# An AdaLN block in one kernel: summing the weights' lower halves on ScalarE in the set-up, and a new order for modulation, transfers and GpSimd work

## The chip, the core and the metric

The kernel runs on one core of one Trainium2 chip. The time is the device time of one execution in microseconds (us), the median of several runs; the profile is one further execution with the hardware profiler on.

## What is computed

The input `x` holds 4 batches of 2048 tokens with 256 channels. Six modulation rows come from a small matrix product, and two sub-layers follow: a chunked delta-rule memory with 4 heads of 64 channels, and a gated feed-forward network (FFN) with hidden layers of 1024.

```python
mod = (silu(c) @ wmod).reshape(4, 6, 1, 256)          # sa, ca, ga, sb, cb, gb
ga, gb = (sign * max(abs, 0.25) of each)
h = layernorm(x) * (1 + ca) + sa
# memory: per head, chunks of 64 tokens, keys rk = h / |h|, wk = rk one token later
A = inv(I + strict_tril(wk wk^T * decay))             # 64 x 64, each chunk and head
v_new = A v - (A wk) S ;  o = rk_g S + intra v_new ;  S = gamma^64 S + wk_g v_new
x = x + ga * (h + (alpha * o) @ Wr.T)
h = layernorm(x) * (1 + cb) + sb
# FFN, weights ternary (-1, 0, 1), scales per output column
f = silu(h W1 s) * (h W2 s); f = gelu(f H1 s); f = gelu(f H2 s)
out = x + gb * (f W3 s)
```

## The kernel before

**Tiling.** A chunk step `s` (0 to 31) holds 64 tokens of all four batches, as 128 partitions by 2 by 256. Two steps make a pair `g` (0 to 15). FFN `g` works on the 512 tokens of pair `g` and runs on TensorE; in its gaps the memory of the next pair is computed, in an order that a small planner (`Beside`, with assumed costs and due times) fixes when the kernel is built. Everything ahead of FFN 0 is the **set-up**: it computes the memory of pair 0 and prepares pair 1, loads weights, and decides one branch.

**The branch.** FFN weights are multiplied in one pass when the lower 16 bits of every fp32 weight are zero, as they are for ternary values. The set-up looks at all of them: `parts` lists 22 pieces of 512 KB (w1, w2, w3, 8 of h1, 8 of h2). `fetch` loads a piece into a staging tile `st`, on ScalarE's queue (ACTq). `look` has ScalarE copy the lower halves to a bf16 tile `low`, which TensorE multiplies by `ones` and adds up in the PSUM row `bad` (two matmuls a piece). `keep` writes an h1 or h2 piece to DRAM (`fh`) in rows of 512 bytes, so that FFN blocks can later be loaded as contiguous tiles `w<-fh`. `bulk` does one of each. At the end `some` and `flag` are formed from `bad`, and every engine loads `flag` and branches.

**The inverse of a pair** goes through four steps. `local_begin` writes `E` to DRAM (`d<-E`) and reads it back as `U` (`U<-d`), both on SyncE's queue (SPq). 31 calls of `local_inverse` (the rows, DVE instructions on `zt` and `Z`) invert blocks of 32. `local_blocks` writes `Z` to DRAM and reads it back (`d<-Z`, `E<-d`, on SPq). `local_diagonal` (`Dm`), `local_merge1` (`yp`, `Y`) and `local_merge2` (`ep`, `E`) finish.

**The recurrence** of a step is `rec_values` (TensorE `V`, ScalarE `vn`), `rec_update` (TensorE `new`, DVE `S` and `oT`), `rec_state` of the next step (TensorE `R` and `O`, DVE `v`), `rec_out` (TensorE `ap_`) and `rec_gain` (DVE `ga`, `y`). `moments` and `ffn_norm` make the FFN's input in `firsts` (tiles named `rkg` and `Dm`); `turn` transposes it (`tpf`) into `hs`. The memory's own inputs are made by `begin`, `local_units` (GpSimd `rk`), `local_keys` (TensorE `tp`), `local_values` (TensorE `vp`), `local_shift` (DMA `wkg<-rk` on SPq), `local_grams` (TensorE `G`, DVE `E` and `IT`), and by GpSimd in `local_residual` (`gh`, `y`), `local_reads` (`rkg`) and `local_writes` (`wkg`).

**What sets the order.** Each engine runs its instructions in one order, fixed at build time. `with stage():` puts its contents behind the last instruction that each engine had been given; inside a stage, and for instructions that are not the last, a scheduler orders. Each queue (SPq, ACTq) issues in its order, and its transfers start in that order. Every DMA also takes one of eight semaphores in turn, and is issued only when the DMA that had that semaphore before it has landed, whichever queue that was on. The tile ring `st` has 10 buffers.

One piece of code matters for the gate in front of the transfers. `first` is a small copy of a result, made only to hold back what stands behind it on ScalarE:

```python
act.copy(first, U[P - K:P, 0, :])
fetch(4)
```

Of the kernel before, what the change touches and what calls it, by code (L numbers as in the profile page):

```python
# [29 lines left out]
F32 = mybir.dt.float32  # L30
# [10 lines left out]
P = 128  # L41
# [48 lines left out]
def adaln_block_kernel(ctx: ExitStack, tc: tile.TileContext, x_in, ww, wr, decay, log_alpha, w1, w2, h1, h2, w3, scol,  # L90
# [80 lines left out]
    def move(out, in_):  # L171
        sp.dma_start(out=out, in_=in_)
# [289 lines left out]
    class Ffn:  # L462
# [151 lines left out]
    with tc.tile_pool(name="setup", bufs=1) as su:  # L614
# [11 lines left out]
        move(out=sk, in_=consts[:, KEPT:NCONST])  # L626
        move(out=kept, in_=consts[:, 0:KEPT])
        move(out=dec[:, 1, :], in_=log_alpha.partition_broadcast(P))
        move(out=wm[1], in_=wmv[:, :, 2 * D:4 * D])
        load(2)  # L630
        move(out=wwT, in_=ww.rearrange("(k p) o -> p k o", p=P))

        parts = [(t, w, k) for t, w in ((fw1, w1), (fw2, w2)) for k in range(NK)]
        parts += [(fw3, w3, k) for k in range(0, NH, 4)] + [(fhs[n], w, k) for n, w in enumerate((h1, h2)) for k in range(NH)]
        staged, seen, gone = [], [], []

        def fetch(count):
            for n in range(count):
                t = su.tile([P, HID], F32, tag="st", name="st", bufs=10)
                _, w, k = parts[len(staged)]  # L640
                staged.append(t)
                k2 = HID // w.shape[1]
                act.dma_start(out=t.rearrange("q (k o) -> q k o", k=k2),
                              in_=w[P * k:P * (k + k2), :].rearrange("(k p) o -> p k o", p=P))

        bad = pf.tile([1, 512], F32, tag="f", name="bad")
        ones = su.tile([P, 1], BF, name="ones")
        dve.memset(ones, 1.0)

        def look(count):  # L650

            for n in range(len(seen), len(seen) + count):
                seen.append(n)
                with stage():
                    low = su.tile([P, HID], BF, tag="low", name="low", bufs=2)
                    act.copy(low, staged[n].bitcast(U16).rearrange("q (o e) -> q o e", e=2)[:, :, 0])
                    for m in range(2):
                        pe.matmul(bad, lhsT=ones, rhs=low[:, 512 * m:512 * m + 512], start=n == 0 and m == 0,
                                  stop=n == len(parts) - 1 and m == 1)

        def keep(count):

            for n in range(count):
                at_ = 6 + len(gone)
                to, w, k = parts[at_]
                gone.append(at_)
                with stage():
                    act.dma_start(out=to[:, :, k, :].rearrange("o p c -> p o c"),
                                  in_=staged[at_].rearrange("q (o c) -> q o c", c=P))

        def bulk(count, more=1):
            for n in range(count):
                look(1)
                keep(1)
                with stage():
                    fetch(min(more, len(parts) - len(staged)))

        def part(at_, n):
            return sk[:, at_ - KEPT:at_ - KEPT + n]
# [18 lines left out]
        def modulation(j):  # L698

            got = []  # L700
            for n in range(2):
                ps = pf.tile([P, 2, D], F32, tag="f", name="ps_mod")
                for k in range(NK):
                    pe.matmul(ps, lhsT=rows(n, k), rhs=wm[j][:, k, :], start=k == 0, stop=k == NK - 1)
                got.append(ps)
            return got
# [53 lines left out]
            got = moments(2)  # L760
        with stage():
            local_values(1, hT1)
        look(8)
        with stage():
            rn = begin(2, got)
        with stage():
# [6 lines left out]
        with stage():  # L773
            first = su.tile([K, K], F32, name="first")
            act.copy(first, U[P - K:P, 0, :])
            fetch(4)
            move(out=wm[2], in_=wmv[:, :, 4 * D:6 * D])
            load(3)
            move(out=wrT[:, 0], in_=wr.rearrange("(k p) o -> p k o", p=P))
            for h in range(2):  # L780
                move(out=wrT[C * (1 - h):C * (1 - h) + C, 1], in_=wr.rearrange("(k h p) o -> h p k o", h=2, p=C)[h])
            s3b = su.tile([P, D], F32, name="s3b")
            move(out=s3b, in_=s3.partition_broadcast(P))
            move(out=sc, in_=scol)
# [10 lines left out]
        with stage():  # L795
            for n, ps in enumerate(modulation(1)):
                act.copy(mod[:, GA, n, :], ps[:, 0, :])
                act.copy(mod[:, SB, n, :], ps[:, 1, :])
        keep(2)
        with stage():  # L800
            hT = local_keys(2, hids[2])
        with stage():
            for n, ps in enumerate(modulation(2)):
                act.activation(mod[:, CB, n, :], ps[:, 0, :], AF.Identity, bias=1.0)
                act.copy(mod[:, GB, n, :], ps[:, 1, :])
        bulk(4, 0)

        def bounded(to):

# [10 lines left out]
        with stage():  # L820
            for n in range(2):
                bounded(mod[:, GA, n, :])
            local_writes(0)
            local_writes(1)
            local_reads(1)
        with stage():
            for n in range(2):
                bounded(mod[:, GB, n, :])
            dve.tensor_tensor(mod[:, GB], mod[:, GB], over(s3b, 1, 2), ALU.mult)
            local_residual(0, hids[0])  # L830
        with stage():
            got = moments(3)
# [1 line left out]
                for n in range(2):  # L834
                    dve.tensor_scalar(wrT[:, n, p, :], wrT[:, n, p, :], alc[:, n, p:p + 1], None, ALU.mult)
        with stage():
            local_diagonal()
            act.copy(first[:, 0:1], Dm[0:K, 1, 7, K - 1:K])
            fetch(6)
        with stage():  # L840
            Y = local_merge1()
        with stage():
            local_merge2(Y)
        bulk(1)
        with stage():
            vn = rec_values(0)
            rn = begin(3, got)
            local_residual(1, hids[1])
        bulk(1)
        with stage():  # L850
            oT = rec_update(0, vn, None)
            local_shift(2)
            local_units(3, hid, rn)
        with stage():
            oT1 = rec_state(1)
        bulk(1)
        with stage():
            vn = rec_values(1)
        with stage():
            a = rec_out(0, oT)  # L860
        with stage():
            rec_gain(0, a, dve)
        with stage():
            oT = rec_update(1, vn, oT1)
        bulk(1)
        with stage():
            got = moments(0)
            local_values(2, hT)
        with stage():
            hT = local_keys(3, hid)  # L870
        with stage():
            a = rec_out(1, oT)
        with stage():
            local_grams(2)
            local_shift(3)
        bulk(1)
        with stage():
            rec_gain(1, a, dve)
        with stage():
            ffn_norm(0, got, firsts[0])  # L880
        bulk(len(parts) - len(seen))
        with stage():
            got = moments(1)
            local_grams(3)
        with stage():
            ffn_norm(1, got, firsts[1])
            local_begin()
            local_residual(2, hids[2])
        with stage():
            local_values(3, hT)  # L890
            local_reads(3)
            local_writes(2)
            local_writes(3)
            local_residual(3, hid)
        some = su.tile([1, 1], F32, name="some")
        dve.tensor_reduce(some, bad, AX.X, ALU.add)
        dve.tensor_scalar(flag, some, 0.0, None, ALU.is_gt)

    val = nc.values_load(flag, min_val=0, max_val=1)

# [9 lines left out]
    class Beside:  # L910
# [14 lines left out]
        def __init__(self, exact, fp, done):  # L925
            self.exact, self.fp, self.hs, self.had = exact, fp, None, {}
            self.t, self.dve, self.act, self.limit, self.gated, self.taken, self.ahead = 0.0, 0.0, 0.0, None, False, False, False
            self.free = {"a1": [0.0], "a2": [0.0, 0.0]}
            self.done = dict.fromkeys(done, -20.0) | {("begin", 1): -4.0}
            self.todo = []  # L930
            for g in range(NP):
                self.pair(g)
            self.todo.sort(key=lambda e: self.RANK.index(f"{e[0][0]}{e[0][1] % 2}" if e[0][0] in ("state", "units") else e[0][0]))
# [133 lines left out]
    SET_UP += [(kind, s) for s in range(2) for kind in ("state", "V", "update", "out", "gain", "fmom", "norm", "turn")]  # L1067
    SET_UP += [("reads", s) for s in (0, 1, 3)] + [("merge2", 0), ("begin", 1)]

    def steps(exact):  # L1070
        for e in engines:
# [66 lines left out]
```

## Time and profile before

| | us |
|---|---|
| median of 3 runs (lowest to highest) | 1753.31 (1750.13 to 1756.47) |
| the profiled execution: its time | 1755.09 |
| its span (first to last instruction) | 1753.3 |
| set-up, until FFN 0's first matmul | 122.9 |
| TensorE busy in the set-up | 64.2 |
| TensorE busy in the 1630.4 behind it | 1602.1 |

A line of the profile names the engine (PE is TensorE, PEld its weight loads, DVE VectorE, ACT ScalarE, POOL GpSimd; SPq and ACTq are issues of DMA), the source line (nearly always 82, the helper that records every operation, so tiles tell instructions apart), the operation, and the tiles as out<-in. TensorE is nearly always busy behind the set-up and half idle in it.

### The profile page before, as it was taken

To read this page: it belongs to the slowest core of one execution; us is meant where nothing else is said; L and a number is where in the kernel's file an instruction comes from. 1 tells how busy PE (TensorE), PEld (TensorE's weight loads), DVE (VectorE), ACT (ScalarE), POOL (GpSimd) and SP (SyncE) were. 2 spreads that over 40 slices of the span, in tenths; PEclk is the share of its full clock that TensorE was granted. 3 is DMA by queue.
4 is the path that set the end of the run, shared out by engine and by line. 5 is a ranking of instruction groups with operands and counts; after the bars stand their busy time and mean duration, and the time that the engine had idled before them with its cause. 6 is when DMAs were issued, how large, how long until landed. Compare 5 with 4: busy or idle time off the path is not lost.

```text
span 1753.3 us, 36864 instructions
## 1 busy us (share of the span) xinstructions
PE 1666.3 (95%) x15236; PEld 1351.2 (77%) x15236; DVE 1001.5 (57%) x2414; ACT 729.9 (42%) x1199; POOL 534.7 (30%) x483
## 2 busy tenths in 40 slices
PE   5379999999999999999999999999999999999998
PEld 2157867878888887888888788888878888887887
DVE  5748484754646566474655657465664746555422
ACT  4334443444444444344443434344343444434342
POOL 3233324141342243324323332422333243231120
PEclk8679999999999999999999999999999999999999
DMA  7765333343433425243352534335253433525142
GB/s 211 235 180 144 92 89 95 94 121 120 131 109 92 140 61 167 82 126 107 96 142 61 158 90 126 110 83 150 64 157 92 116 114 86 146 65 150 61 133 86
DMA packets 189874, 205.46 MB, mean 117 GB/s; under 512 B 112576, under 2 KB 147520, under 8 KB 189696
## 3 DMA queue, kind: packets, MB, share of 16 engines
q10 hardware_dynamic: 57712, 154.68, 28.4%
q1 hardware_dynamic: 131984, 48.32, 12.6%
q8 instruction: 122, 2.00, 0.5%
q14 instruction: 56, 0.46, 0.1%
HBM read 169.40 MB, written 25.17 MB: 111 GB/s over the span
## 4 chain that ended last, share of the span: by engine, by line
PE 88%; DVE 5%; DMA 3%; ACT 1%; issue 1%; SPq 1%; POOL 0%; ACTq 0%; DVEq 0%; POOLq 0%
PE ps L82 70%; PE vp L82 3%; PE new L82 2%; DVE Z L82 2%; PE tp L82 2%; DVE zt L82 2%; PE V L82 1%; PE R L82 1%; PE ep L82 1%; PE G L82 1%; DVE raw L82 1%; PE O L82 1%; DMA d<-Z 1%; PE tpf L82 1%; PE yp L82 1%
## 5 line engine op out<-in xcount | busy, mean ns | idle before, releaser
L82 PE MATMUL ps<-act,w 128*128 128x512 f32 x4096 | 987.4, 396 | 14.8 <-DVE act L82 13.7
L82 PEld LDWEIGHTS ps<-act,w 128*128 128x128 f32 x4096 | 759.8, 188 | 181.0 <-DVE act L82 19.7
L82 ACT ACTIVATE raw<-ps,sc 128x512 f32<-128x512 f32 x384 | 264.7, 689 | 634.8 <-PE ps L82 629.2
L82 DVE TENSOR_TENSOR act<-raw,act 128x512 fp32r<-128x512 f32 x272 | 195.2, 718 | 218.1 <-ACT act L82 215.9
L82 ACT CAST act<-raw 128x512 fp32r<-128x512 f32 x384 | 237.7, 619 | 56.8 <-DVE raw L82 48.8
L82 PE MATMUL ps<-hs,fw 128*128 128x512 f32 x1024 | 246.5, 399 | 3.6 <-DVE raw L82 2.6
L82 PEld LDWEIGHTS ps<-hs,fw 128*128 128x128 f32 x1024 | 191.0, 189 | 53.7 <-DVE raw L82 5.6
L82 POOL TENSOR_TENSOR act<-raw,act 128x512 fp32r<-128x512 f32 x112 | 143.3, 1295 | 130.9 <-ACT act L82 130.9
L82 DVE TENSOR_TENSOR Z<-Z,zt 128x126 f32<-128x126 f32 (+22 forms) x496 | 161.9, 326 | 17.2
L82 DVE SCALAR_TENSOR_TENSOR raw<-ps,sc,raw 128x512 f32<-128x512 f32 x128 | 95.9, 749 | 110.7 <-PE ps L82 55.5
L82 POOL TENSOR_TENSOR rs<-rs,half 128x2 f32<-128x2 f32 x64 | 51.5, 805 | 338.9 <-DVE rs L82 338.2
L82 DVE TENSOR_TENSOR zt<-Z,U 128x126 f32<-128x126 f32 (+22 forms) x496 | 138.4, 279 | 16.4 <-DMA U<-d 4.5
L82 PE MATMUL ps<-fw,act 128*128 128x256 f32 x1024 | 125.6, 280 | 1.4 <-DVE act L82 1.4
L82 PEld LDWEIGHTS ps<-fw,act 128*128 128x128 f32 x1024 | 122.8, 188 | 4.0 <-DVE act L82 2.7
L82 POOL TENSOR_TENSOR y<-y,gb 128x512 f32<-128x512 f32 x30 | 39.5, 1318 | 234.6 <-DVE gb L82 234.6
L82 POOL TENSOR_TENSOR rn<-rn,half 128x8 f32<-128x8 f32 x32 | 53.9, 1683 | 141.0 <-DVE rn L82 140.3
L82 DVE SCALAR_TENSOR_TENSOR S<-S,gC,new 128x256 f32<-128x256 f32 x64 | 27.8, 476 | 84.3 <-PE new L82 84.3
L82 DVE BATCH_NORM_STATS2 bs<-y 128x6 f32<-128x256 f32 x128 | 47.8, 414 | 42.9 <-POOL y L82 37.0
L82 ACT ACT_TABLE_LOAD x35 | 44.9, 1283 | 64.0 <-PE ps L82 50.6
L82 PE MATMUL vp<-wwT,hT 128*128 128x256 f32 x256 | 65.8, 401 | 4.8 <-DMA wwT<-in_ww_dram 4.8
L82 POOL TENSOR_TENSOR rk<-hid,rn 128x512 f32<-128x512 f32 x32 | 34.8, 1087 | 99.2 <-DMA wkg<-rk 97.9
L82 POOL TENSOR_TENSOR y<-y,ga 128x512 f32<-128x512 f32 x30 | 40.2, 1340 | 78.2 <-DVE ga L82 78.2
(205 smaller groups left out, 1377.1 us busy)
## 6 DMA issues: line engine op xcount, KB each, us to landing
w<-fh ACTq DMA_DIRECT2D x256, 512.0 KB, 3.7
y<-in_x_dram SPq DMA_DIRECT2D x64, 128.0 KB, 4.2
st<-in_h_dram ACTq DMA_DIRECT2D x16, 512.0 KB, 5.9
U<-d SPq DMA_DIRECT2D x32, 256.0 KB
fh<-st ACTq DMA_DIRECT2D x16, 512.0 KB, 6.2
out_dram<-y SPq DMA_DIRECT2D x64, 128.0 KB, 2.4
wkg<-rk SPq DMA_DIRECT2D x64, 126.0 KB
d<-E SPq DMA_DIRECT2D x64, 64.0 KB, 1.9
```

Of the source, the lines that this page charges most:

```text
L82: made = make(*args, **kwargs)
```

## The change

It touches the set-up, the list of what the planner takes as done, and one due time.

- `look`: ScalarE's instruction adds up along each partition as it copies (`accum_out`), into a column of `sums`; the 44 `bad` matmuls become two small ones with `sums`, and `low` becomes six tiles.
- `wm[1]`, 512 KB for modulation rows, is loaded behind `local_begin`'s stage instead of early. `modulation(2)` stands behind the 31 rows and `local_blocks`; bounding `GB` stands behind `rec_values(1)`.
- `st` gets 12 buffers. The pieces of h1 behind the first 12 are loaded and kept on SPq, behind `local_blocks`; the pieces of h2 are loaded and looked at, but their copy to `fh1` goes from DRAM to DRAM, eight transfers on SPq in the last stage.
- The order of the recurrence and of steps 2 and 3 changes: `local_values(2)` and `local_keys(3)` stand ahead of `rec_out(0)`; both `local_grams` together.
- `local_residual(3)`, `local_writes(2)`, `local_writes(3)`, `local_reads(3)` are left to the planner, which puts them at the start of FFN 0. `begin` of pair 1 counts as done at -2 instead of -4.

```diff
-        move(out=wm[1], in_=wmv[:, :, 2 * D:4 * D])
...
-        def fetch(count):
+        def fetch(count, by=act.dma_start):
...
-                t = su.tile([P, HID], F32, tag="st", name="st", bufs=10)
+                t = su.tile([P, HID], F32, tag="st", name="st", bufs=12)
...
-                    low = su.tile([P, HID], BF, tag="low", name="low", bufs=2)
-                    act.copy(low, staged[n].bitcast(U16).rearrange("q (o e) -> q o e", e=2)[:, :, 0])
-                    for m in range(2):
-                        pe.matmul(bad, lhsT=ones, rhs=low[:, 512 * m:512 * m + 512], start=n == 0 and m == 0,
-                                  stop=n == len(parts) - 1 and m == 1)
+                    act.activation(lows[n % 6], staged[n].bitcast(U16).rearrange("q (o e) -> q o e", e=2)[:, :, 0],
+                                   AF.Copy, accum_out=sums[:, n:n + 1])
...
-        look(8)
+        look(6)
...
             act.copy(first, U[P - K:P, 0, :])
             fetch(4)
+            move(out=wm[1], in_=wmv[:, :, 2 * D:4 * D])
             move(out=wm[2], in_=wmv[:, :, 4 * D:6 * D])
...
-        keep(2)
+        keep(4)
         with stage():
             hT = local_keys(2, hids[2])
-        with stage():
-            for n, ps in enumerate(modulation(2)):
...
-        bulk(4, 0)
+        look(3)
...
         with stage():
+            local_diagonal()
+            act.copy(first[:, 0:1], Dm[0:K, 1, 7, K - 1:K])
+            fetch(4, move)
+        keep(2, move)
+        with stage():
+            fetch(2, move)
+        with stage():
+            Y = local_merge1()
             local_residual(0, hids[0])
...
         with stage():
             oT = rec_update(0, vn, None)
             local_shift(2)
             local_units(3, hid, rn)
+            local_residual(2, hids[2])
+        look(1)
+        keep(2, move)
+        with stage():
+            fetch(4, move)
...
         with stage():
             vn = rec_values(1)
+        look(2)
+        with stage():
+            for n in range(2):
+                bounded(mod[:, GB, n, :])
+            dve.tensor_tensor(mod[:, GB], mod[:, GB], over(s3b, 1, 2), ALU.mult)
+        with stage():
+            local_values(2, hT)
+        with stage():
+            hT = local_keys(3, hid)
+        look(6)
...
-        bulk(len(parts) - len(seen))
         with stage():
             got = moments(1)
-            local_grams(3)
+            local_values(3, hT)
+        with stage():
+            pe.matmul(bad[:, 6:len(parts)], lhsT=ones, rhs=sums[:, 6:], start=True, stop=True)
         with stage():
             ffn_norm(1, got, firsts[1])
+        some = su.tile([1, 1], F32, name="some")
+        with stage():
+            dve.tensor_reduce(some, bad[:, 0:len(parts)], AX.X, ALU.add)
+            dve.tensor_scalar(flag, some, 0.0, None, ALU.is_gt)
+        with stage():
             local_begin()
-            local_residual(2, hids[2])
-        with stage():
-            local_values(3, hT)
-            local_reads(3)
-            local_writes(2)
-            local_writes(3)
-            local_residual(3, hid)
...
+            for k in range(NH):
+                move(out=fhs[1][:, :, k, :], in_=h2[k * P:(k + 1) * P, :].rearrange("p (o c) -> o p c", c=P))
...
-            self.done = dict.fromkeys(done, -20.0) | {("begin", 1): -4.0}
+            self.done = dict.fromkeys(done, -20.0) | {("begin", 1): -2.0}
...
-        "load", "mom", "hidden", "squares", "sizes", "units", "residual", "keys", "values", "shift", "writes", "gram")]
+        "load", "mom", "hidden", "squares", "sizes", "units", "keys", "values", "shift", "gram")]
+    SET_UP += [("residual", s) for s in range(3)]
...
```

Built, the change gives these orders, which the diff alone does not show. On ACTq the four `fetch(4)` transfers stand ahead of the `first` copy that reads `U`. On SPq the eight `fh1<-h2` transfers stand behind `local_shift(3)` and ahead of pair 1's `d<-E`. Behind the branch TensorE's order is the same as before; on DVE the inverse's rows of pair 1 begin one `raw` instruction later.

More of the change, by code (lines that the diff above doesn't have):

```diff
@@ L634, in adaln_block_kernel @@
         parts += [(fw3, w3, k) for k in range(0, NH, 4)] + [(fhs[n], w, k) for n, w in enumerate((h1, h2)) for k in range(NH)]
-        staged, seen, gone = [], [], []
-        def fetch(count):
+        staged, seen, known, gone = [], [], [], []
+        def fetch(count, by=act.dma_start):
             for n in range(count):
-                t = su.tile([P, HID], F32, tag="st", name="st", bufs=10)
+                t = su.tile([P, HID], F32, tag="st", name="st", bufs=12)
                 _, w, k = parts[len(staged)]
@@ L642, in fetch, with keep @@
                 k2 = HID // w.shape[1]
[L643 to L648, printed above, removed]
+                by(out=t.rearrange("q (k o) -> q k o", k=k2),
+                   in_=w[P * k:P * (k + k2), :].rearrange("(k p) o -> p k o", p=P))
+        ones = su.tile([P, 1], F32, name="ones")
+        lows = [su.tile([P, HID], BF, name=f"low{n}") for n in range(6)]
+        sums = su.tile([P, len(parts)], F32, name="sums")
+        dve.memset(sums, 0.0)
         def look(count):
             for n in range(len(seen), len(seen) + count):
+                with stage():
+                    act.activation(lows[n % 6], staged[n].bitcast(U16).rearrange("q (o e) -> q o e", e=2)[:, :, 0],
+                                   AF.Copy, accum_out=sums[:, n:n + 1])
                 seen.append(n)
-                with stage():
-                    low = su.tile([P, HID], BF, tag="low", name="low", bufs=2)
-                    act.copy(low, staged[n].bitcast(U16).rearrange("q (o e) -> q o e", e=2)[:, :, 0])
-                    for m in range(2):
-                        pe.matmul(bad, lhsT=ones, rhs=low[:, 512 * m:512 * m + 512], start=n == 0 and m == 0,
-                                  stop=n == len(parts) - 1 and m == 1)
-        def keep(count):
+        def keep(count, by=act.dma_start):
             for n in range(count):
@@ L667, in keep @@
                 with stage():
[L668 to L674, printed above, removed]
-                with stage():
-                    fetch(min(more, len(parts) - len(staged)))
+                    by(out=to[:, :, k, :].rearrange("o p c -> p o c"),
+                       in_=staged[at_].rearrange("q (o c) -> q o c", c=P))
         def part(at_, n):
@@ L798, in adaln_block_kernel @@
                 act.copy(mod[:, SB, n, :], ps[:, 1, :])
-        keep(2)
+        keep(4)
         with stage():
             hT = local_keys(2, hids[2])
-        with stage():
-            for n, ps in enumerate(modulation(2)):
-                act.activation(mod[:, CB, n, :], ps[:, 0, :], AF.Identity, bias=1.0)
-                act.copy(mod[:, GB, n, :], ps[:, 1, :])
-        bulk(4, 0)
+        look(3)
         def bounded(to):
@@ L820, in adaln_block_kernel @@
         with stage():
+            pool.memset(ones, 1.0)
+        bad = pf.tile([1, 512], F32, tag="f", name="bad")
+        with stage():
+            pe.matmul(bad[:, 0:6], lhsT=ones, rhs=sums[:, 0:6], start=True, stop=True)
+        with stage():
+            for n, ps in enumerate(modulation(2)):
+                act.activation(mod[:, CB, n, :], ps[:, 0, :], AF.Identity, bias=1.0)
+                act.copy(mod[:, GB, n, :], ps[:, 1, :])
+        with stage():
             for n in range(2):
@@ L826, in adaln_block_kernel @@
         with stage():
-            for n in range(2):
-                bounded(mod[:, GB, n, :])
-            dve.tensor_tensor(mod[:, GB], mod[:, GB], over(s3b, 1, 2), ALU.mult)
+            local_diagonal()
[6 more added lines that the diff above has]
+            Y = local_merge1()
             local_residual(0, hids[0])
@@ L836, in adaln_block_kernel @@
         with stage():
[L837 to L842, printed above, removed]
             local_merge2(Y)
-        bulk(1)
+            local_residual(1, hids[1])
         with stage():
@@ L847, in adaln_block_kernel @@
             rn = begin(3, got)
-            local_residual(1, hids[1])
-        bulk(1)
         with stage():
@@ L853, in adaln_block_kernel @@
             local_units(3, hid, rn)
+            local_residual(2, hids[2])
[3 more added lines that the diff above has]
+            fetch(4, move)
         with stage():
             oT1 = rec_state(1)
-        bulk(1)
         with stage():
             vn = rec_values(1)
+        look(2)
[5 more added lines that the diff above has]
+            local_values(2, hT)
+        with stage():
+            hT = local_keys(3, hid)
+        look(6)
         with stage():
@@ L864, in adaln_block_kernel @@
             oT = rec_update(1, vn, oT1)
-        bulk(1)
+        with stage():
+            local_shift(3)
         with stage():
             got = moments(0)
-            local_values(2, hT)
-        with stage():
-            hT = local_keys(3, hid)
+            masks = [local_grams(2, False), local_grams(3, False)]
         with stage():
             a = rec_out(1, oT)
+            ffn_norm(0, got, firsts[0])
         with stage():
-            local_grams(2)
-            local_shift(3)
-        bulk(1)
+            for n in range(2):
+                for m in range(2):
+                    masks[n](m)
+        look(22 - len(seen))
         with stage():
@@ L879, in adaln_block_kernel @@
         with stage():
-            ffn_norm(0, got, firsts[0])
-        bulk(len(parts) - len(seen))
+            got = moments(1)
+            local_values(3, hT)
         with stage():
-            got = moments(1)
-            local_grams(3)
+            pe.matmul(bad[:, 6:len(parts)], lhsT=ones, rhs=sums[:, 6:], start=True, stop=True)
         with stage():
             ffn_norm(1, got, firsts[1])
-            local_begin()
-            local_residual(2, hids[2])
-        with stage():
-            local_values(3, hT)
-            local_reads(3)
-            local_writes(2)
-            local_writes(3)
-            local_residual(3, hid)
-        some = su.tile([1, 1], F32, name="some")
-        dve.tensor_reduce(some, bad, AX.X, ALU.add)
-        dve.tensor_scalar(flag, some, 0.0, None, ALU.is_gt)
+        some = su.tile([1, 1], F32, name="some")
+        with stage():
+            dve.tensor_reduce(some, bad[:, 0:len(parts)], AX.X, ALU.add)
+            dve.tensor_scalar(flag, some, 0.0, None, ALU.is_gt)
+        with stage():
+            local_begin()
+            for k in range(NH):
+                move(out=fhs[1][:, :, k, :], in_=h2[k * P:(k + 1) * P, :].rearrange("p (o c) -> o p c", c=P))
     val = nc.values_load(flag, min_val=0, max_val=1)
@@ L1065, in adaln_block_kernel @@
     SET_UP = [(kind, s) for s in range(4) for kind in (
-        "load", "mom", "hidden", "squares", "sizes", "units", "residual", "keys", "values", "shift", "writes", "gram")]
-    SET_UP += [(kind, s) for s in range(2) for kind in ("state", "V", "update", "out", "gain", "fmom", "norm", "turn")]
-    SET_UP += [("reads", s) for s in (0, 1, 3)] + [("merge2", 0), ("begin", 1)]
+        "load", "mom", "hidden", "squares", "sizes", "units", "keys", "values", "shift", "gram")]
+    SET_UP += [("residual", s) for s in range(3)]
+    SET_UP += [(kind, s) for s in range(2) for kind in ("reads", "writes", "state", "V", "update", "out", "gain", "fmom",
+                                                        "norm", "turn")]
+    SET_UP += [("merge2", 0), ("begin", 1)]
     def steps(exact):
```

## The prediction

> **What bounds the kernel now.** I read busy time by stage first, then the chain of waits through the set-up, then the timeline. Columns of the stages: length, busy time (instructions) of PE, PEld, DVE, ACT, POOL, then granted clock, DMA share, GB/s.
>
> ```profile
> 44.20:62.20 18.00, 8.62 (x26) 3.08 (x25) 15.85 (x63) 8.57 (x22) 0.00 (x0) 0.79 1.01 312
> 62.20:76.40 14.20, 0.00 (x0) 0.00 (x0) 12.27 (x28) 0.19 (x1) 10.71 (x9) 0.50 0.73 229
> 76.40:122.90 46.50, 31.72 (x516) 21.63 (x517) 21.91 (x45) 17.39 (x26) 11.71 (x14) 0.72 0.64 185
> 122.90:225.00 102.10, 100.66 (x981) 81.14 (x982) 64.49 (x163) 45.67 (x74) 34.65 (x31) 0.98 0.39 109
> ```
>
> From 122.9 us PE is full, and its order there is unchanged. So the change is worth what FFN 0's start moves, less what FFN 0 then waits. The set-up's chain (start, us, what):
>
> ```profile
> 62.97 9.14 DMA d<-Z
> ...
> 82.38 1.05 ACT low L82
> 83.47 1.01 PE bad L82 x2
> 84.49 1.11 PE V L82 x32
> ...
> 93.50 1.06 ACT low L82
> 94.59 1.01 PE bad L82 x2
> 95.61 1.06 PE V L82 x32
> ```
>
> The 2048 rows of `d<-Z` take 9.1 us; then V and new stand behind `bad` matmuls, which wait for ScalarE's copies. The timeline names both other costs:
>
> ```profile
> 12.89 0.87 DVE L82 SCALAR_TENSOR_TENSOR hid<-hid,rs,mod 128x256 f32<-128x256 f32 x2
> ...
> 44.20 1.78 ACTq L82 DMA_DIRECT2D st<-in_h_dram  x4
> ...
> 59.97 2.20 ACTq L82 DMA_DIRECT2D st<-in_h_dram  x4
> ...
> 118.07 2.81 DVE L82 SCALAR_TENSOR_TENSOR Dm<-Dm,rs,mod 128x256 f32<-128x256 f32 x2
> ...
> 132.74 0.18 DVE L82 TENSOR_TENSOR zt<-Z,U 128x31 f32<-128x31 f32 x1
> ```
>
> Fetches go out at 59.97 just ahead of `d<-Z` (62.24), and the last norm takes 2.81 where the same instructions took 0.87, beside GpSimd's `gh`, `y` and `rkg`.
>
> **Step 1, until U lands (44.2): 4.0 later.** `wm[1]` leaves the early loads and joins SPq's line ahead of `d<-E`: 512 KB at 399 GB/s (31 to 32 us) is 1.3. The early loads get shorter; DMA was saturated there (share above 1.0 from 14 to 23), and I give the chain through `rk` 0.6 back. The fetch of four pieces (2.1 MB) no longer stands behind the copy that reads U. The four wait only for wrT, sc and the first two `d<-E`, so they run beside `d<-E` and `U<-d`. All in front of them at the 390 GB/s of such fetches would cost 5.4, none 0; `d<-Z` above shows that small rows lose most beside 4 KB rows. Two or three of the four overlap: 3.3. Bounds 0.7 to 6.1. The 31 rows take 18.0 as before. `look` keeps its price, 1046 ns a piece; adding up may cost some tenths of a us a piece, which ScalarE's idle time (17.39 busy of 46.5) covers.
>
> **Step 2, d<-Z: 4.5 earlier.** No fetch stands ahead: `keep(4)` is 2.1 MB at 346 GB/s, 6 us from U on, over before the rows end. From 62.24 to `E<-d` at 72.17 is 9.9; later pairs need 5.6, 5.4, 4.6 and 6.4 (159.92 to 165.52, 472.98 to 478.35, 577.72 to 582.33, 257.71 to 264.08). I take 5.4; bounds 3.5 to 5.3 gained. `modulation(2)` moves off the rows to PE and ACT that are idle from 62 to 76 (0.00 and 0.19 busy); its `bounded` of GB (67.35 to 71.2, 3.9) goes between two DVE waits (oT and `ga`, 7.25 idle). Merge 1 moves from 76.4 to 75.9; call it B.
>
> **Step 3, from B to FFN 0's first matmul (46.5 before): 37.9, so 8.6 earlier.** V starts behind E's copy (82.36, not 84.42), new behind vn (86.21, not 88.14), V of step 1 behind O (92.95, not 95.53): 2.1, 1.9 and 2.6 saved, V ends at B+13.7. Then PE runs vp, moved ahead (1.99 at full clock, 3.52 at 0.50; a mixture, 2.7), two `tp` groups (0.6 each) and `ap_` (2.0): B+19.6. `tp` needs rk of step 3, which waits for `wkg<-rk`; that now stands on SPq behind 4.2 MB of fetch and keep, 11 to 12 us from B+1.5, so rk comes at B+16, about when PE gets there. From B+19.6 DVE is the chain: ga, y 1.4; S and oT 1.5; moments 1.3; norm 0 1.7; four masks 2.8; ga, y 1.4; moments and GpSimd's power 2.0; the rest of norm 1 0.9, uncontended; flag 0.4. That is B+33.0. Loading the flag and branching: SPq's lines behind the flag take 0.7. Two turns follow one another on one PSUM tile (tpf 0.66, ACT 0.59, DVE 0.68, tpf 0.66, ACT 0.59 and hops): 3.7. With 0.5 for a branch that norm 1 no longer hides: B+37.9. Bounds 36.9 to 40.5: a branch that costs 2 more, or rk 1 later.
>
> Start of FFN 0: 122.9 + 4.0 - 4.5 - 8.6 = 113.8, 9.1 earlier.
>
> **Step 4, inside FFN 0.** GpSimd's five extra instructions (1.2 to 1.3 each, 6.4 with the gaps) lie between the branch and its first `act<-raw`, 5.4 behind the first matmul (128.37 against 122.91) and some 9 behind the branch: nothing. U of pair 1 is the open price. SPq issues eight DRAM-to-DRAM transfers (4.2 MB in 512-byte rows) ahead of `d<-E`, when `local_shift(3)` is out, and that waits for new of step 1 (B+20.8) and the last fetches: data from B+24.3, for a time T. Then `d<-E` and `U<-d`, 7.9 as before (36.44 to 44.2, which bounds queueing). DVE stands still at the first row if U is late, and the `raw` instructions that free PE's PSUM tiles are queued behind it. Row 0 was 9.8 behind the first matmul (132.74); one `raw` later, 11.5, or B+49.4. So U is late from T = 17.2, and DVE's slack from 130 to 160 (3.4 idle of 30) and three PSUM tiles give some 3 back: FFN 0 loses T - 20. No transfer of before goes from DRAM to DRAM. The nearest row is the `keep` stream from 53 to 62, also 512-byte rows, at 339 GB/s: T = 12.4, nothing lost. From the other side, reads of 1 and 2 KB rows ran at 214 GB/s (32 to 33 us) on all engines, and the 63-row `wkg<-rk` filled 0.43 to 0.65 of them (91.4 to 92.2 us): 214 GB/s on half the engines is T = 39, 19 lost. I take the `keep` row, nearest in size, rows and direction of the write.
>
> The Trainium skill ("DMA: Bandwidth & Descriptors", "Why a DMA increments its semaphore by 16 and not by 1") lets a transfer use the largest number of engines up to 16 that divides the slowest dimension of both patterns. The 63 rows' share agrees with its 9. The source pattern here begins with a dimension of 8, so by the rule T would be an estimated 24.8, FFN 0 would lose 4.8, and the sum would be 1750; the rule speaks against the change, and no DRAM-to-DRAM transfer of this trace tests it.
>
> **Sum.** 1755.1 (the profiled execution, span 1753.3 and 1.8 around it) - 9.1 = 1746.0. It lies 1.8 above the median of three; from the median the sum is 1744.2. I give 1745.
>
> **Rivals.**
> - Slower: the copies hold U. From T = 29 they eat the gain; by T = 36 (233 GB/s on half of the engines) FFN 0 loses 16: 1761. For: they stand ahead of `d<-E` on one queue, and the source is read in short pieces. Against: the `keep` stream at 339 GB/s.
> - No change, by the copies: T near 25, half the engines at the `keep` stream's price, 4.8 lost: 1750.
> - No change, by the gate: all four fetches pass `d<-E` (6.1 instead of 4.0), `d<-Z` gains 3.5 instead of 4.5, the late rk and the branch cost 2 more: 1750. For: 9.14 for `d<-Z` beside fetches. Against: the semaphores' turns hold two of the four until `d<-E` lands.
> - Faster still: the fetches miss `d<-E` (0.7 instead of 4.0): 1742.
>
> **How the numbers follow.** The measurement tells about 0.3% (5.3 us) from no change: faster is below 1748.0, slower above 1758.6. Chances: forecast 0.43 (1742 to 1750), faster still 0.06, gate 0.15, copies at T near 25 0.12, slow copies 0.24. Faster: nearly all of the first (0.40), the second, a third each of the two middle ones (0.09): 0.55. Slower: the last and a little: 0.25. Same: 0.20. Range: 1740 takes in the faster case and the forecast's lower bounds; 1760 takes in both middle cases and the nearer part of the slow one; 0.16 stays out.
>
> **What would show it.** First `zt` at 48 (44.3 before); `d<-Z` to `E<-d` near 5.4; V right behind E's copies; the last norm at 0.9 a pair; FFN 0's first matmul near 114; the first `zt` of pair 1 waiting on `U<-d` by less than 1 us. A wait of 10 or more there, with PE idle behind it, proves the slower rival. First matmul past 118 proves steps 1 to 3 wrong.

## The result, and the profile after

The change takes 1757.2 us (median of 16 runs, 1753.6 to 1761.1) against 1753.8 for the kernel before (16 runs, 1750.1 to 1757.1): a ratio of 1.0019, 95% interval 1.0011 to 1.0028. It is some 3.4 us slower, inside the 0.3% that I called no change and inside the range, but not the gain that I forecast. The profiled execution of the change has a span of 1756.6 us (1753.3 before), so the two profiles can be set against each other almost as they stand.

The stages of the change, cut at the same events as before (first row, last row, merge 1, FFN 0's first matmul) and one more, the turn of step 2. Columns: length, busy time (instructions) of PE, PEld, DVE, ACT, POOL, then granted clock, DMA share, GB/s.

```profile
50.30:68.30 18.00, 0.00 (x0) 0.00 (x0) 15.89 (x63) 5.81 (x16) 0.00 (x0) 0.50 0.41 117
68.30:76.30 8.00, 6.06 (x13) 2.37 (x15) 5.69 (x11) 1.37 (x5) 6.19 (x7) 0.69 0.40 61
76.30:115.60 39.30, 26.24 (x498) 20.35 (x498) 25.77 (x63) 21.08 (x42) 14.23 (x15) 0.68 0.81 253
115.60:213.70 98.10, 90.79 (x852) 72.45 (x853) 53.53 (x138) 39.57 (x65) 33.63 (x32) 0.94 0.49 138
```

The rows take 18.0 as before. The stretch from them to merge 1 has shrunk from 14.2 to 8.0, and the next from 46.5 to 39.3, although PE stood at a granted clock of 0.68. FFN 0 pays: 98.1 to the turn of step 2, where the kernel before needed 90.1 for the same 852 matmuls:

```profile
122.90:213.00 90.10, 88.66 (x852) 70.62 (x853) 56.03 (x138) 39.38 (x65) 34.10 (x31) 0.98 0.43 121
```

The chain of waits of the change, where it differs (start, us, what):

```profile
41.31 8.91 DMA U<-d
...
69.06 2.88 DMA d<-Z
...
81.17 1.18 PE V L82 x32
...
87.88 4.89 DMA wkg<-rk
...
101.53 3.72 PE ap__938 L82 x8
...
106.03 3.80 PE vp L82 x8
```

`d<-Z` is 2.88 instead of 9.14, and V follows merge 2 without a `bad` matmul between. But `U<-d` of pair 0 took 8.91, where the chain of the kernel before has

```profile
40.21 3.96 DMA U<-d
```

PE waits for rk behind `wkg<-rk`; `ap_` and vp run at half clock (1.99 at full). The timeline shows why, and what PE loses by it:

```profile
39.69 0.82 ACTq L82 DMA_DIRECT2D st<-in_h_dram  x2
...
100.72 23.19 SPq L82 DMA_DIRECT2D fh<-in_h_dram  x8
...
108.88 0.88 DVE L82 SCALAR_TENSOR_TENSOR Dm<-Dm,rs,mod 128x256 f32<-128x256 f32 x2 [0.19 <-POOL rs L82]
...
124.02 5.26 SPq L82 DMA_DIRECT2D d<-E  x4
131.62 1.19 SPq L82 DMA_DIRECT2D U<-d  x2
136.64 0.19 DVE L82 TENSOR_TENSOR zt<-Z,U 128x31 f32<-128x31 f32 x1 [8.51 <-DMA U<-d]
138.29 2.08 PE L82 MATMUL ps<-hs,fw 128*128 128x512 f32 x4 [7.29 <-DVE raw L82]
```

The first of them are the last two ungated fetches, just ahead of `U<-d`; norm 1's last pair is at 0.88. SPq needed 23.19 us to issue the eight copies of h2; `d<-E` could go out at 124.0 only, DVE stood 8.51 in front of pair 1's first row, and PE 7.29 in front of the `raw` that is queued behind that row.

Where the 3.3 us between the two profiles lie:

| stretch | before | after | difference | forecast |
|---|---|---|---|---|
| start to first row | 44.3 | 50.3 | +6.1 | +4.0 |
| first row to merge 1 | 32.2 | 25.9 | -6.2 | -4.5 |
| merge 1 to FFN 0's first matmul | 46.5 | 39.4 | -7.1 | -8.6 |
| FFN 0's first matmul to the turn of step 3 | 96.4 | 104.4 | +8.0 | 0 |
| turn of step 3 to turn of step 7 | 183.7 | 186.4 | +2.7 | 0 |
| the rest | 1350.3 | 1350.1 | -0.1 | 0 |

### The profile page after: what moved, and what is told of

The parts are those of the page before. It is cut to its first block, busy times and chain, and to the rows that moved or that the text cites. A ratio compares the mean times of both kernels' runs of the same rounds, so it can differ in the third digit from the quotient of the medians.

```text
span 1756.6 us, 36796 instructions
## 1 busy us (share of the span) xinstructions
PE 1658.1 (94%) x15196; PEld 1352.0 (77%) x15196; DVE 995.8 (57%) x2414; ACT 731.6 (42%) x1221; POOL 532.0 (30%) x484
## 4 chain that ended last, share of the span: by engine, by line
PE 86%; DVE 6%; DMA 4%; issue 1%; SPq 1%; ACT 1%; POOL 0%; ACTq 0%; DVEq 0%; POOLq 0%
PE ps L82 69%; PE vp L82 3%; PE new L82 2%; DVE Z L82 2%; PE tp L82 2%; DVE zt L82 2%; PE V L82 1%; PE R L82 1%; PE G L82 1%; PE ep L82 1%; SPq L82 1%; DVE raw L82 1%; PE tpf L82 1%; PE O L82 1%; DMA U<-d 1%
## 5 line engine op out<-in xcount | busy, mean ns | idle before, releaser
L82 PE MATMUL ps<-hs,fw 128*128 128x512 f32 x1024 | 249.0, 401 | 10.1 <-DVE raw L82 9.2
L82 DVE TENSOR_TENSOR Z<-Z,zt 128x126 f32<-128x126 f32 (+22 forms) x496 | 159.9, 322 | 17.2
L82 DVE SCALAR_TENSOR_TENSOR raw<-ps,sc,raw 128x512 f32<-128x512 f32 x128 | 95.9, 750 | 112.2 <-PE ps L82 57.1
L82 PEld LDWEIGHTS ps<-fw,act 128*128 128x128 f32 x1024 | 122.9, 188 | 4.0 <-DVE act L82 2.7
```

What stands on the lines that cost most here:

```text
L82: made = make(*args, **kwargs)
```

## The experiments

Theory: the set-up's gain is real, and two transfers eat it: the copies of h2, which use half of the DMA engines ahead of pair 1's U, and the ungated fetch, which makes pair 0's `U<-d` late. Rivals: copies from DRAM to DRAM are slow by their short reads; `wm[1]` ahead of `d<-E` is what delays U; the gain is lost again at a later wait.

What the profiles and times of all runs say (us; ratio to the kernel before, with its 95% interval):

| run | first row | merge 1 | FFN 0 starts | to turn of step 3 | median time | ratio |
|---|---|---|---|---|---|---|
| before | 44.3 | 76.4 | 122.9 | 96.4 | 1753.8 | |
| the change | 50.3 | 76.3 | 115.6 | 104.4 | 1757.2 | 1.0011 to 1.0028 |
| e1 | 51.0 | 76.9 | 114.9 | 96.6 | 1748.6 | 0.9968 to 0.9986 |
| e2 | 49.2 | 75.1 | 113.1 | 96.7 | 1750.9 | 0.9977 to 0.9995 |
| e3 | 44.7 | 70.7 | 108.9 | 104.2 | 1752.0 | 0.9980 to 0.9998 |
| e4 | 44.4 | 70.3 | 108.2 | 96.0 | 1746.5 | 0.9950 to 0.9977 |
| e5 | 45.0 | 77.8 | 116.4 | 97.5 | 1748.6 | 0.9954 to 0.9980 |
| e6 | 46.2 | 72.2 | 111.5 | 96.8 | 1745.9 | 0.9937 to 0.9966 |
| e7 | 45.4 | 71.3 | 112.2 | 96.3 | 1745.6 | 0.9940 to 0.9970 |
| e8 | 45.2 | 72.1 | 109.3 | 96.1 | 1745.5 | 0.9935 to 0.9964 |
| e9 | 44.7 | 76.2 | 113.7 | 97.3 | 1750.9 | 0.9960 to 0.9982 |
| e10 | 45.4 | 71.8 | 108.7 | 97.0 | 1743.7 | 0.9921 to 0.9949 |

**e1: the copies on all engines.**

```
-   move(out=fhs[1][:, :, k, :], in_=h2[k * P:(k + 1) * P, :].rearrange("p (o c) -> o p c", c=P))
+   move(out=fhs[1][:, :, k, :].rearrange("o p c -> p o c"),
+        in_=h2[k * P:(k + 1) * P, :].rearrange("p (o c) -> p o c", c=P))
```

> The change with one edit: the eight copies of h2 from DRAM to DRAM have their two patterns turned round, so that both begin with 128 rows instead of 1024 and 8; bytes, piece size and place in the queue stay. Theory (half the DMA engines carried the copies, and they hold U of pair 1): the copies take 12 to 14 us instead of 23 to 25, DVE's 8.5 us wait for U of pair 1 is under 1, PE's gaps in front of R of FFN 0 fall from 7.3 to under 1, the turn of step 2 comes near 206 (213.7 in the change, 213.0 before), and the time is 1749 (1747 to 1751), 8 less than the change's 1757.2. Rival (a copy from DRAM to DRAM is slow by its 512-byte reads, whatever the engines): 23 us and 1757 again. Second rival (what FFN 0 gains is lost again at merge 1 of pair 3, where PE waited 2.1 us in the change's profile): the turn of step 2 at 206 but a time of 1753 or more.

The stretch of the copies, first in the change, then here, by windows (columns as above):

```profile
108.00:128.00 20.00, 16.53 (x115) 11.82 (x114) 6.83 (x13) 8.03 (x12) 11.33 (x13) 0.67 0.57 170
```

```profile
106.00:116.00 10.00, 6.54 (x20) 4.35 (x21) 5.07 (x14) 3.88 (x6) 5.86 (x9) 0.67 0.98 283
```

And the timeline of e1:

```profile
100.72 12.62 SPq L82 DMA_DIRECT2D fh<-in_h_dram  x8
...
126.89 0.95 DVE L82 TENSOR_TENSOR zt<-Z,U 128x31 f32<-128x31 f32 x1
```

Share 0.57 and 170 GB/s became 0.98 and 283: 4.2 MB in an estimated 15 us (4.19 MB at 283 GB/s) instead of 25 (at 170). The first row of pair 1 no longer waits for a transfer, FFN 0 is back to 96.6, and the time is 8.7 less. A packet of 512 bytes took 27 to 28 ns on its engine in both (the share of 16 engines, times 512 bytes, over the rate), so the engines were not slower in the change, half of them were missing. The theory holds; the first rival falls.

**e2: the copies behind U of pair 1, still on half of the engines.**

```
             local_begin()
-
+        with stage():
             for k in range(NH):
```

> The change with the eight copies put behind the transfers of U of pair 1 on SPq; they still use half of the engines. Theory (it is their place ahead of d<-E that costs): U lands before FFN 0 begins, no wait for it, turn of step 2 near 206, time 1749 (1747 to 1751), although the copies still take 23 to 25 us; their target is first read in FFN 0's second hidden layer, some 40 us later. Rival (the copies' traffic, not their place, slows what is beside them): U lands on time but w<-fh or y comes late, PE waits, and the time stays above 1753.

The timeline of e2:

```profile
106.46 1.16 SPq L82 DMA_DIRECT2D U<-d  x2
107.66 21.45 SPq L82 DMA_DIRECT2D fh<-in_h_dram  x8
...
125.22 0.95 DVE L82 TENSOR_TENSOR zt<-Z,U 128x31 f32<-128x31 f32 x1
```

The copies take as long as before, and nobody waits for them: FFN 0 96.7. So the cost is the product of two things, half of the engines and the place ahead of U, and either edit removes it.

**e3: the fetch behind ScalarE's copy that reads U.**

```
             act.copy(first, U[P - K:P, 0, :])
-            fetch(4)
-            move(out=wm[1], in_=wmv[:, :, 2 * D:4 * D])
+        with stage():
+            fetch(4)
+        with stage():
+            move(out=wm[1], in_=wmv[:, :, 2 * D:4 * D])
```

> The change with the fetch of four pieces in a stage of its own behind ScalarE's copy that reads U, as it stood in the kernel before. Copies of h2 as in the change. Theory (the fetch beside U<-d is what made that transfer 8.9 us instead of 4.3): U<-d back at 4 to 5 us, first row at 45.5 to 46.5 (50.3 in the change, 44.3 before), everything behind it 4 to 4.8 earlier, FFN 0's first matmul at 111, its wait for U of pair 1 as long as in the change; time 1752.7 (1751.5 to 1754). Rival (wm[1] on SPq ahead of d<-E is the cause): first row at 49.5 or later, time 1757. Second rival (the fetch now collides with d<-Z or holds look and keep): first row at 46 but merge 1 gains less than 2 us, time 1755 to 1757.

The timeline of e3:

```profile
44.64 0.21 ACT L82 COPY first<-U 32x32 f32<-32x32 f32 x1 [7.00 <-DMA U<-d]
44.64 1.78 ACTq L82 DMA_DIRECT2D st<-in_h_dram  x4
44.71 0.19 DVE L82 TENSOR_TENSOR zt<-Z,U 128x31 f32<-128x31 f32 x1 [4.86 <-DMA U<-d]
```

The first row is at 44.7, 5.6 earlier than in the change, and `U<-d` takes 4.1 instead of 8.9. `wm[1]` still stands ahead of `d<-E` here, and the first row is only 0.4 later than in the kernel before: that rival falls. So does the second: merge 1 comes 5.6 earlier as well, at 70.7. FFN 0 starts 6.7 earlier and loses the same 8 to the copies. Time 5.2 less than the change.

**e4: both edits** (the diffs of e1 and e3).

> Both edits: the copies' patterns on all engines, and the fetch behind the copy that reads U. Theory: the two costs lie in different stretches and add up: FFN 0 starts near 111 and loses nothing to U, turn of step 2 near 201.5, time 1744.5 (1743 to 1747), 0.5 per cent under the kernel before. Rival (a later wait takes part of it back): turn of step 2 near 201.5, but a time above 1748.

FFN 0 starts at 108.2 and loses nothing. In the profiled executions the two gains add up: 1758.7 in the change, 1748.6 in e1 and 1751.9 in e3 (10.1 and 6.8 less), 1742.1 here (16.6 less). In the medians they do not: 8.7 and 5.2, and 10.7 together from five runs. The profiled execution of e4 is the fastest of its five, that of the change is 1.4 above its median. Which stretches are slower in the other runs of e4 no profile shows.

**e5: the kernel before, with the sums alone.**

```
-    act.copy(low, staged[n]...)
-    for m in range(2):
-        pe.matmul(bad, lhsT=ones, rhs=low[:, 512 * m:512 * m + 512], ...)
+    act.activation(low, staged[n]..., AF.Copy, accum_out=sums[:, n:n + 1])
...
+    pe.matmul(bad[:, 0:len(parts)], lhsT=ones, rhs=sums, start=True, stop=True)
```

> The kernel before with one part of the change alone: ScalarE sums the lower halves while it copies them, and one matmul at the end takes the place of the two behind each piece. Order, fetches, copies of h2 and GpSimd's work stay as before. Theory (V and new stood behind the bad matmuls, 2.1 + 1.9 + 2.6 us): merge 1 starts at 76.4 as before, FFN 0 starts 5 to 7 us earlier (116 to 118, before 122.9) and loses none of it; time 1748 (1746.5 to 1749.5). Rival (ScalarE, not PE, is what V waits for: its copies of 1.05 us, now 1.2, stand ahead of the copies of E, vn and oT): FFN 0 starts less than 2.5 earlier, time 1751.5 or more.

The chain of waits of e5 around V, and ScalarE's timeline there:

```profile
83.72 0.03 ACT E L82
83.80 1.17 PE V L82 x32
```

```profile
84.73 0.19 ACT L82 ACTIVATION_READ_ACCUMULATOR low<-st 128x1 f32 x1
```

V follows the copy of E. The sum adds an instruction of 0.19 us a piece on ScalarE; where several pieces follow one another, they come every 1.04 us in the change, 0.95 in the kernel before. Merge 1 to FFN 0 takes 38.5 instead of 46.5: this part alone gives all of what the change gains there. Merge 1 was 1.4 later in this profile, and the time is 1748.6, as expected. Nothing else in the change was needed for that stretch.

**e6: `wkg<-rk` of step 2 ahead of two keeps and two fetches** (base e4).

```
             fetch(4, move)
-        keep(2, move)
-        with stage():
-            fetch(2, move)
...
             local_residual(2, hids[2])
+        keep(2, move)
+        with stage():
+            fetch(2, move)
```

> The change with copies on all engines and the gated fetch (the best so far), and SPq's order turned round at one place: the transfers wkg<-rk of step 2 ahead of two keeps and two fetches of set-up pieces, that stood in front of them. Theory (the late rk costs what PE waited at tp, 1.3 us): rk of step 3 comes 3 to 4 us earlier, PE waits 0 at tp, FFN 0 starts 1.0 to 1.5 earlier, time 1.3 less than without (about 1745). Rival (the pieces that now come later hold the looks and the flag): FFN 0 starts at the same time or later.

The timeline of e6:

```profile
104.46 1.06 ACT L82 ACTIVATE low<-st 128x1024 bf16<-128x1024 uint16 x1 [0.64 <-DMA st<-in_h_dram]
...
105.66 0.21 PE L82 MATMUL bad<-sums,ones 128*1 128x16 f32 x2 [2.34 <-ACT low L82]
```

PE no longer waits at tp, but the pieces that were pushed back came last: the last look waits for its fetch, the flag for the look, and merge 1 to FFN 0 takes 39.3 (37.9 in e4). The rival was right: the wait for rk turned into a wait for the flag. The time is the same within the intervals.

**e7: GpSimd's work back in the set-up** (base e4).

```
             ffn_norm(1, got, firsts[1])
+            local_reads(3)
+            local_writes(2)
+            local_writes(3)
+            local_residual(3, hid)
```

(The planner's list of what is done is changed to fit.)

> The same best kernel with the GpSimd work that the change left to FFN 0 (writes of steps 2 and 3, reads and residual of step 3) back in the set-up, beside norm 1. Theory (DVE's norm is slower beside GpSimd's large instructions): norm 1's pairs take 1.8 to 2.8 us instead of 0.88, FFN 0 starts 1 to 2.5 us later, time 1 to 2.5 more than without. Rival (the norm's end is covered by the flag and the branch): FFN 0 starts within 0.4 of before, time unchanged.

The timeline of e7:

```profile
104.01 1.17 POOL L82 TENSOR_TENSOR rkg<-keys,gpT 128x512 f32<-128x512 f32 x1
104.07 2.57 DVE L82 SCALAR_TENSOR_TENSOR Dm<-Dm,rs,mod 128x256 f32<-128x256 f32 x2 [0.19 <-POOL rs L82]
```

The pair of DVE instructions takes 2.57 beside `rkg` (0.88 in the change) and merge 1 to FFN 0 is 40.9 (37.9 in e4), which is the way the theory says. Only 1.7 of these 3.0 are the pair: `ap_` of step 1 and vp of step 3 took 3.78 each here, and 3.33 and 1.99 in e4. The Trainium skill ("SBUF — State Buffer", "SBUF: two separate sides") has GpSimd and a VectorE instruction with two SBUF inputs lock one port pair in turn; these rows agree with it. But the time did not rise: 1745.6 beside e4's 1746.5. On the time this run is inconclusive: the two intervals overlap, and a profile is one execution.

**e8 and e9: the next fetch beside `d<-Z` again** (base e4). First on ScalarE's queue in front of the stage of `d<-Z`, with nothing that holds it:

```
+        with stage():
+            fetch(4)
         with stage():
             local_blocks()
...
-            fetch(4, move)
```

> The same best kernel with the fetch of the next four pieces back on ScalarE's queue just ahead of d<-Z (in the change it stands behind E<-d). Theory (2.1 MB of 4 KB rows beside d<-Z's 128-byte rows made that transfer 9.1 us before, 2.9 after): d<-Z takes 7 to 9 us again, merge 1 starts 5 to 6 us later (75.5 to 76.5), FFN 0 3.5 to 5.5 later, since rk no longer waits for that fetch; time 3.5 to 5.5 more than without. Rival (d<-Z was slow by something else, the keeps still on the queue): it stays under 4 us, time unchanged.

The four were issued from 55.4 to 58.6, all of them more than 4.5 us ahead of `d<-Z`, which then took 3.74 (2.88 in e4). So it tested little of what it was meant to, and the time did not rise. Then behind a copy that reads the last row's Z:

```
+        with stage():
+            act.copy(first[:, 1:2], Z[0:K, K // 2 - 1, K - 1:K])
+        with stage():
+            fetch(4)
...
-            fetch(4, move)
```

> Once more the fetch of four pieces beside d<-Z, since the last attempt put it out 5 us ahead of d<-Z instead of beside it: here ScalarE first copies a column of Z that the last row writes, and issues the fetch behind that, so that it leaves together with d<-Z. Base: copies on all engines, gated fetch. Theory (4 KB rows beside the 128-byte rows stretch d<-Z): 7 to 9 us instead of 2.9, merge 1 some 4 to 6 later, FFN 0 3 to 5 later, time 1748 to 1751. Rival (what made d<-Z slow before was the six pieces together with the keeps ahead of them on that queue, four alone do not): under 4.5 us, time 1746.

The chains of waits, e8 and then e9:

```profile
63.90 3.74 DMA d<-Z
```

```profile
63.47 8.23 DMA d<-Z
```

Four fetches that leave together with it stretch `d<-Z` from 2.9 (e4) to 8.2, merge 1 comes 5.5 later than in e4 relative to the first row (31.4 against 25.9), and the median is 4.3 above e4's. For the transfer the theory holds: when the fetch leaves is what costs. For the time it is less certain, since the intervals of the two ratios overlap.

**e10: what the runs point to** (e2's and e8's edits on e4).

> What the runs point to, together: copies on all engines and behind U of pair 1, the fetch of four gated behind the copy that reads U, the next four fetched on ScalarE's queue ahead of the end of the rows. Theory: U of pair 1 lands before FFN 0 begins, nothing waits; 1744 to 1745.5, that is 0.5 per cent under the kernel before. Rival: with U no longer late nothing is left to gain, and the copies beside w<-fh cost: 1746.5 or more.

1743.7 us, the lowest median of the study: 0.9935 of the kernel before (0.9921 to 0.9949) and 13.5 us under the change. Its interval lies just below e4's and overlaps those of e6, e7 and e8. FFN 0 starts at 108.7.

**e11: a smaller first dimension** (base e2, one execution).

```
-    move(out=fhs[1][:, :, k, :], in_=h2[k * P:(k + 1) * P, :]...)
+    for n in range(0, NH, 4):
+        move(out=fhs[1][n:n + 4, :, k, :],
+             in_=h2[k * P:(k + 1) * P, n * P:(n + 4) * P].rearrange("p (o c) -> o p c", c=P))
```

> The change with the copies behind U of pair 1, cut into sixteen whose source begins with a dimension of 4 (8 in the change, 128 in the repaired one). Theory (the share of engines follows that dimension): DMA share near 0.28, about 85 GB/s, 4.2 MB in 46 to 52 us, 27 ns a row as before. Rival (8 engines is what any DRAM to DRAM copy in this order gets): share 0.56 and 25 us as before.

Windows of e2, then of e11:

```profile
112.00:128.00 16.00, 15.32 (x115) 11.41 (x113) 6.91 (x11) 8.62 (x13) 9.94 (x9) 0.82 0.58 175
```

```profile
112.00:144.00 32.00, 16.42 (x123) 12.42 (x121) 9.50 (x19) 7.40 (x12) 8.88 (x7) 0.77 0.29 87
```

Share 0.29 and 87 GB/s: half of e2's. With first dimensions of 128, 8 and 4 the share is 0.98, 0.57 and 0.29. (Its time, 1770.7, is another matter: ScalarE stood 21.9 us at its queue in front of a `w<-fh`, and FFN 0 took 121.8.)

## Why the prediction was wrong

The forecast was 1745, 9.1 us faster in the profile's terms. Its last step failed; three others were mis-sized.

- **Step 4, the copies: this failed.** I priced them by the `keep` row (12.4 us), the nearest in size, rows and direction of the write. They took some 25. What decides, the first dimension of the pattern, was not among the features by which I called a row near. The Trainium skill's rule ("DMA: Bandwidth & Descriptors", "Why a DMA increments its semaphore by 16 and not by 1"), which I weighed and set aside, gave an estimated 24.8, and the three shares of e1, e2 and e11 agree with it.
- **What a late U costs** was too low even in the rival that had T near 25: it gave 4.8, since DVE's slack and three PSUM tiles were to give 3 back. U was late by 8.5, PE stood 7.3, and FFN 0 lost 8.0: of the 3 only 0.5 came back. It is partly luck that 8.5 is near this rival's 7.8 (25 - 17.2), as two errors nearly cancel: U was there at B+60.3, where the sum gives B+57.2, and DVE was ready for the row at B+51.8, not B+49.4. That rival came nearest in its mechanism; the slow rival (T from 29) had the place right and the rate wrong.
- **Step 1 was mis-sized:** +6.1 instead of +4.0, the upper bound. `wm[1]` and the shorter early loads cost 0.4 (e3), not 0.7; the fetch cost 5.6, not 3.3. I had two or three of the four pieces pass beside `d<-E`; in the profile the last two went out at 39.7 and together the four delayed `U<-d`, which rose from 4.1 (e3) to 8.9. From 41 to 46 us ScalarE's queue still moved 1.65 MB of the 2.1, and SPq, with `U<-d`, 0.16 MB (view of DMA): my own bound, all four in front for 5.4, was the nearer one.
- **Step 2 was right in its mechanism and mis-sized the other way:** from `d<-Z`'s issue to `E<-d`'s it is 3.7 (68.32 to 71.99), not the 5.4 of later pairs, so that 6.2 was gained and not 4.5. Merge 1 is at 76.3, 75.9 foretold, because the errors of steps 1 and 2 almost cancel, which is luck. e9 shows the cause.
- **Step 3 was right in its mechanism and 1.5 short:** V behind E's copy, norm 1's last pair at 0.88. From merge 1 to FFN 0 it is 39.4 where I had 37.9; e1 to e4, in which PE's granted clock there was 0.71 to 0.77 instead of 0.68, show 37.9 to 38.3. In the change both `ap_` of step 1 and vp of step 3 ran at half clock (3.7 and 3.8 instead of 2.0), in each of e1 to e4 only one of them, wholly or for the most part (3.2 to 3.7). That goes with the 1.5; I had counted half clock for vp of step 2 alone (2.7, it took 2.1). e5 shows that the sums alone carry this step.
- **Between the turns of steps 3 and 7** the change lost 2.7, which no step had: there E's transfers of pair 3 landed late and PE waited. Behind the turn of step 7 nothing changed, as forecast.

The stretch between these turns takes 183.7 to 187.8 us over the thirteen profiles, in the same order on PE, and it follows the granted clock there and PE's waits for E. At 1.00 (e1, e2, e7) it is 183.7 to 184.1, with PE busy for 176.4; at 0.99 (the change, e3, e4, e8) 185.9 to 186.4, with 178.0 or 178.1; at 0.98 (e5, e6, e9, e10, e11) 185.4 to 187.8, with 179.2 to 179.6 (in e6 and e11, the shortest of these, PE does not wait at pair 2's merge 1). The kernel before, at 0.99, needed only 183.7: in its profile alone PE does not wait for E of pair 3 (0.5 to 1.7 in front of the first `yp` in the twelve others). So most of the change's 2.7 is this wait, 2.1 with two short ones behind it, and not the clock.

What stays open is why E lands later there in all the other kernels, also in e5, whose order is that of before. That was not tested, and with one profile of the kernel before chance is not excluded. The medians, which differ by 3.4, fit a wait that is there in most executions better than the 0.7 that is left without it.

## What to carry to other kernels

A transfer that is moved off the engines' path still has a rate and a place in its queue: look at the first dimension of both patterns before taking a price from another transfer of the same size, and see what stands behind it on the queue. Transfers on the critical chain paid here for each bulk transfer that left at the same moment (e3, e9), so tie the bulk to an event behind them, not ahead. Where a change bundles five edits, the one that carries the gain (here the sums, 8 us) may need none of the others.

## What the runs showed of the hardware that I had not expected

- A copy from DRAM to DRAM takes an engine no longer for 512 bytes than a store from SBUF: 27 to 28 ns at each of the three shares and in the `keep` stream. On all engines it ran at 283 GB/s, beside the 339 of that stream.
- It is not only short rows that suffer beside bulk: `U<-d`, 128 rows of 4 KB, went from 4.1 to 8.9 beside 2.1 MB in rows of the same length, while `d<-E` with its 128-byte rows, which left before them, took 3.2 as in the kernel before. What was lost is near the time that the bulk still needed. The four pieces are an estimated 5.4 us at the 390 GB/s of step 1; beside all four the first row came 5.6 later (the change against e3) and `d<-Z` took 5.3 more (e9 against e4), and with the four issued more than 4.5 us ahead it took 0.9 more (e8).
- A short wait of PE can cost twice. In pair 3 of the change PE waited 2 us for E (timeline):

```profile
356.91 1.38 DVE L82 STREAM_TRANSPOSE Dm<-E 128x256 f32<-128x256 f32 x3 [3.92 <-DMA E<-d]
...
357.42 0.25 PE L82 MATMUL yp<-Dm,E 32*32 32x32 f32 x4 [1.71 <-DVE Dm L82]
...
359.13 4.61 PE L82 MATMUL ps<-act,w 128*128 128x512 f32 x12
```

  and the twelve matmuls behind merge 1, which have no gap, took 4.61 where the kernel before needed 3.00: from 360.0 to 363.4 the granted clock was 0.50, although PE had been busy for 2.07 of the 3.4 us before. In e1 PE waited 1.23 at the same place, and the same twelve took 3.04 at a granted clock of 1.00. What decides between the two no run here shows.
